# A fused attention and feed-forward block: second layernorm in pairs ahead of q, half of the second v in front of the branch, maxima on two PSUM rings, third layernorm among k

## The chip, the cores and the metric

The kernel runs on one core of a Trainium2 chip. The metric is the device time of one execution in microseconds (us). The core's engines are TensorE (PE; its weight loads are listed as PEld), VectorE (DVE), ScalarE (ACT), GpSimd (POOL) and SyncE (SP, which here issues nearly all DMA). Each runs its own instructions in the order of the program and waits on semaphores for the others.

## The reference

The input x is 16 batches of 512 tokens by 512 channels, in float32. There is one block of a transformer with "sandwich" layernorms:

```python
x = x + layernorm(attention(layernorm(x), Wq, bq, Wk, bk, Wv, bv, Wo, bo))
x = x + layernorm(ffn(layernorm(x), gate_w, up_w, down_w, gate_s, up_s, down_s))
```

Attention has 32 heads of 16 channels, two rotary turns of q and k (they are one fixed rotation per token), a causal mask and a softmax over 512 keys. The feed-forward part computes `silu(g) * u` with `g = (x @ gate_w.T) * gate_s` and `u` likewise, over 1408 hidden channels, then the down product times `down_s`. The weights of the feed-forward part are drawn from -1, 0 and 1.

## The kernel before, in words

**The parts.** `front` (line 765) does the first layernorms and batch 0's q, k and v. Then the program branches (line 845), and `batches` (line 863) does everything else. In the branch that runs here, the feed-forward products take each float32 operand as a sum of two rounded parts (`exact`). The branch is taken on a flag: `check_weights` (line 193) rounds each of the 22 weight pieces on ACT and compares on DVE (11 pieces of 128x1024 for gate and up, 11 of 128x512 for down), then `total` adds up the differences, and each engine reads the flag from memory. The pieces are loaded by `load_checks` (line 170) into places that are free at first, `ht` and `xntfl` among them.

**A q or k block** (`qk_block`, line 326) makes 128 channels for 512 tokens: four products on TensorE, each a pair of records in the trace (`pq`, `pk`). ACT then writes `ys` (the bias added, halves swapped), DVE `ya`, POOL multiplies `ys` by the sine. That is the block's tail; `rest` adds the two on DVE, rounds on ACT to `yh`, and takes the remainder on POOL as `yl`; `store` sends both to DRAM (`qd`, `kd`). `ya` and `ys` have one buffer each, so the next block's tail waits for this one's rest.

**A layernorm of 128 tokens**: `stats` (line 235) has three instructions on DVE and two on POOL (a power, `ln_rstd`, and a shift, `ln_sh`). Then one instruction writes `xn`, on DVE in `front` and on ACT (`scaled`) later. `turn` (line 253) transposes it with four products `px` on TensorE, and ACT copies them out to `xnta` (or `xntf`).

**In the front** the second batch's layernorm is spread over the first batch's four q blocks: each block is followed by a check, a layernorm, and three more checks. The second batch's `xn`, transposed, goes to DRAM (`xn1`) and is read back behind the branch. TensorE's products pass through `ps_d`, three PSUM buffers in turn.

**Steps.** Behind the branch the work is a list of steps, six for each group of four heads, eight groups per batch (`one_step`, line 749). A step issues, for a group, a sixth of the score products: those of `st` (keys by queries, for the exponentials `pt`), and those of `s` of the next group but one or the next (queries by keys, for the row maxima `nm`). `s` and `st` each have one buffer of two PSUM banks (`ps_s`, `ps_t`). DVE masks and reduces each `s` (`maxima`, line 606); once per group the maxima are transposed (`pm`) and sent by SP to where the `st` products of that group read them (`mx`). ACT's exponentials are masked on POOL, then multiplied by v (`av`). The steps of n = -2 and n = -1 are a ramp: they have `s` alone, for the first two groups.

**The lists.** Into each step, after the scores, `run_list` (line 691) puts a share of a list of dense work, by cost: 1 for a product, 0.15 for a transpose. In the list, `merge` places a function after so much cost, and `("need", key)` forces a named one. The first list, `dense(0) + ffn_list(None, 2)`, makes v, q and k of batch 1, a product of the biases (`fold_bias`, `po`), and at its end the third batch's layernorms and transposes one after the other. It is spread over 58 of the 60 steps of the ramp and batch 0. The lists after it, for batches 1 to 15, hold the next batch's v, q and k and the previous batch's output product and feed-forward part.

**Loads.** SP issues all loads and stores in program order, and each waits for its own buffers and data: `load_group` (q, kh, kl of one group) at the first step of two groups earlier, weights `w` (four buffers), the copies `wgs` of the gate and up weights, maxima and stores between them. One that waits holds up all that follow.

Of the kernel before, what the change touches and what calls it, by code (L numbers as in the profile page):

```python
# [18 lines left out]
P = 128  # L19
T = 512  # L20
# [34 lines left out]
class Block:  # L55
# [53 lines left out]
    def constants(self):  # L109
        nc, a, con = self.nc, self.a, self.const  # L110
        for tb in range(NB):
            self.load_x(0, tb, ("x", "xr")[tb // 2], 2)
        ncol = sum(n for _, n in a["cols"][1])
        cols = con.tile([P, ncol], FP, tag="cols", name="cols")
        self.sp.dma_start(out=cols, in_=a["cols"][0])
        self.col, at = {}, 0
        for name, n in a["cols"][1]:
            self.col[name] = cols[:, at : at + n]
            at += n
        turn = con.tile([P, 2, T], FP, tag="turn", name="turn")  # L120
        self.cos, self.sin = turn[:, 0, :], turn[:, 1, :]
        nc.scalar.dma_start(out=turn, in_=a["turn"])
        for name in "qk":
            for half in range(2):
                self.load_w(0, name, half)
        for tb in range(NB):
            self.load_x(1, tb, "x1", 4)
        self.ident = con.tile([P, P], FP, tag="ident", name="ident")
        make_identity(nc, self.ident)
        self.neghalf = con.tile([P, 1], FP, tag="neghalf", name="neghalf")  # L130
        nc.gpsimd.memset(self.neghalf, -0.5)
        self.row = {}
# [14 lines left out]
        self.v17 = []  # L147
        for i in range(2):
            t = con.tile([P, NB, WIDTH], FP, tag=f"v17_{i}", name=f"v17_{i}")
            self.v17.append(t)  # L150
        self.one = con.tile([P, P], FR, tag="one", name="one")
        nc.vector.memset(self.one.bitcast(FP), 1.0)
        self.qd, self.kd, self.od, self.rd = [], [], [], []
        for par in range(2):
            for c in range(NC):
                self.qd.append(self.dram.tile([P, 2, T], FP, tag=f"qd{par}{c}", name="qd"))
                self.kd.append(self.dram.tile([2, P, T], FP, tag=f"kd{par}{c}", name="kd"))
                self.od.append(self.dram.tile([8 * 32, T], FP, tag=f"od{par}{c}", name="od"))
                self.rd.append(self.dram.tile([8, T], FP, tag=f"rd{par}{c}", name="rd"))
        self.wgs = self.dram.tile([self.NF, P, 2, NC, P], FP, tag="wgs", name="wgs")  # L160
        self.wds = self.dram.tile([self.F, C], FP, tag="wds", name="wds")
        self.wd = con.tile([P, self.NF, C], FR, tag="wd", name="wd")
        self.xn1 = self.dram.tile([P, NC, T], FP, tag="xn1", name="xn1")
        self.odd = con.tile([P, 2 * self.NF], FP, tag="odd", name="odd")
        self.flag = con.tile([1, 1], mybir.dt.int32, tag="flag", name="flag")
        self.ones = con.tile([P, 1], FP, tag="ones", name="ones")
        nc.vector.memset(self.ones, 1.0)


    def load_checks(self):  # L170

        a, n = self.a, 2 * NC * P
        ht = self.tile([P, self.NF, T], "ht", bufs=1).rearrange("p f t -> p (f t)")
        xl = self.tile([P, NC, T], "xntfl", bufs=1).rearrange("p c t -> p (c t)")
        places = [ht[:, ts(i, n)] for i in range(self.NF * T // n)] + [xl[:, ts(i, n)] for i in range(NC * T // n)]
        small = [tag for tag, k in (("oc", 4), ("q2", 3), ("kh", 3), ("kl", 3)) for _ in range(k)]
        self.wgu0, self.wd0 = [], []

        def load(f):
            w = places.pop() if 3 <= f < 10 else self.tile([P, n], "wf", bufs=3)  # L180
            self.sp.dma_start(out=w, in_=a["wgu"][f].rearrange("p w c j -> p (w c j)"))
            self.wgu0.append(w)

        for f in range(self.NF):
            if f < 10:
                load(f)
            tag = small.pop()
            w = self.tile([P, C], tag, bufs=4 if tag == "oc" else 3)
            self.sp.dma_start(out=w, in_=a["wd"][ts(f, P), :])
            self.wd0.append(w)  # L190
        self.load_check_10 = load

    def check_weights(self):

# [5 lines left out]

        def gate_up(f):
            if f == 1:
                self.load_check_10(10)
            w = self.wgu0[f]
            check(f, w, self.tile(list(w.shape), "pt", bufs=4, dtype=FR))

# [7 lines left out]
            self.pe.matmul(p[0:1, 0:1], n, self.ones, start=True, stop=True)  # L214
            self.dve.tensor_copy(self.flag, p[0:1, 0:1])

        return [lambda f=f, g=g: g(f) for f in range(self.NF) for g in (gate_up, down)] + [total]

    def load_x(self, b, tb, tag="x", bufs=2):
        t = self.tile([P, C], tag, bufs=bufs)  # L220
# [32 lines left out]
    def turn(self, tiles, key, tb, to, big):  # L253
# [3 lines left out]
        def go(c):  # L257
# [3 lines left out]
            if c == NC - 1:  # L261
# [7 lines left out]
                    self.dve.tensor_tensor(lo, p, hi, ALU.subtract)  # L269
                    return  # L270
                if tb == 0:
                    to[key] = self.tile([P, NC, T], big, bufs=1)
                self.act.copy(to[key][:, :, ts(tb, P)], p)

        return [(TR, lambda c=c: go(c)) for c in range(NC)]
# [217 lines left out]
    def dense(self, b):  # L493
# [10 lines left out]
            self.merge(L, rest, 3)  # L504
            self.merge(L, store, 5.5)

        if b == 0:
            do(self.load_xn1)
            for half in range(2):
                do(self.load_w, 1, "v", half)  # L510
        if nxt:
            for tb in range(NB):
                L += self.v_block(bn, tb)
                if b == 0 and tb < 2:
                    do(self.load_w, 1, "q", tb)
            for c in range(NC):
                if c < 2:
                    do(self.load_w, o, "o", c)
# [20 lines left out]
        for c in range(NC):  # L539
# [6 lines left out]
                    self.merge(L, later[c], 5, ("f", c + 2))  # L546
            if nxt:
                qk("k", c)
        if not old:
            L += self.fold_bias()  # L550
        return L


# [10 lines left out]
            ks.append(t)  # L564
        self.qs[n], self.ks[n] = q, ks

    def scores(self, n, m, third, pair):

        ps = pm = None
        todo = []  # L570
        if 0 <= n < self.B * NG:
# [11 lines left out]
                        (out, self.one[r2, :], mx[r2, T - w : T], False, True),  # L583
                    ]
        if 0 <= m < self.B * NG:
            pm = self.ps_s.tile([P, 2, T], FP, tag="s", name="s")
            q, ks = self.qs[m], self.ks[m]
            for jj in range(2):
                j = 32 * (2 * (1 - pair) + jj)
# [159 lines left out]
    def one_step(self, work, n, i):  # L749
# [2 lines left out]
        third, pair = divmod(i, 2)  # L752
        if i == 0 and n + 2 < self.B * NG:
            self.load_group(n + 2)
        self.scores(n, n + 2 if third >= 1 else n + 1, third, pair)
# [9 lines left out]
    def front(self):  # L765
# [8 lines left out]

        def norm(b, tb):
            xt = self.xts.pop((b, tb))
            r, sh = self.stats(xt)

            def rest():
                xn = self.xns[("a", b), tb] = self.tile([P, C], "xn", bufs=2)  # L780
                self.dve.tensor_scalar(xn, xt, r, sh, ALU.mult, ALU.add)

            return rest

# [10 lines left out]
            rest = now  # L795
        rest()
        turn(0, NB - 1)
        for t in self.v17:
            self.pool.memset(t, 0.0)
            self.pool.memset(t[:, :, DH : H * W : W], 1.0)  # L800
        rests, pending = [], []
        for name in "qk":
            for c in range(NC):
                items, rest, store = self.qk_block(0, name, c)
                for _, f in items[:2]:
                    f()
                for f in pending:
                    f()
                for _, f in items[2:3]:
                    f()  # L810
                for f in rests:
                    f()
                items[3][1]()
                rests, pending = [rest, store], []
                if name == "q":
                    check(1)
                    r = norm(1, c)
                    check(1)
                    r()
                    pending = [lambda c=c: turn(1, c)]  # L820
                    check(2)
                else:
                    check(4)
            if name == "q":
                for half in range(2):
                    self.load_w(0, "v", half)
            else:
                t = self.xnts.pop(("a", 1))
                self.sp.dma_start(out=self.xn1, in_=t)
        for f in rests:  # L830
            f()
        check(len(checks))
# [2 lines left out]
        for tb in range(NB):  # L835
            for _, f in self.v_block(0, tb):
                f()
            if tb == 0:
                checks.pop(0)()

    def run(self):
        self.front()
# [19 lines left out]

    def batches(self):
        B = self.B
        L = self.dense(0) + self.ffn_list(None, 2)
        if self.exact:
            for f in range(self.NF):
                L.insert(8 + 5 * f, (0, lambda f=f: self.sp.dma_start(out=self.wgs[f], in_=self.a["wgu"][f])))
        work = self.run_list(L, 58)
        for n in (-2, -1):  # L870
            for i in range(STEPS):
                self.one_step(work, n, i)
        for b in range(B):
            if b:
# [71 lines left out]
```

## Time and profile before

| | |
|---|---|
| median of 3 runs | 3362.67 us (3357.67 to 3367.87) |
| the profiled execution's own time | 3362.85 us |
| its span, first to last instruction | 3360.9 us |
| PE busy | 3143.6 us (94% of the span) |
| DVE busy | 2057.0 us (61%) |
| ACT busy | 1528.9 us (45%) |
| POOL busy | 1360.9 us (40%) |
| mean granted TensorE clock | 0.969 |

Times in the timeline count from the start of the span. Its lines give start, length, engine, operation, output and inputs, and in square brackets how long the engine was idle before, and what ended that. Lines of waits give who waited for whom: us in total, times, the longest. Lines of stages give a stretch, its length, the busy time of PE, PEld, DVE, ACT and POOL with their instructions, the granted clock of TensorE as a share of full speed, the busy share of the DMA engines and the GB/s moved. In the strip of the page, each digit is a fortieth of the span (84 us): busy tenths, or tenths of the full clock. Almost every instruction is issued through one helper, line 50, so groups are told apart by their tiles.

### The profile page before, as it was taken

The numbers are of one execution on the slowest core, as the hardware profiler recorded it, in microseconds if no ns is written. First come the engines' busy times: TensorE is split into PE (matmuls) and PEld (weight loads), VectorE is DVE, ScalarE is ACT, GpSimd is POOL, SyncE is SP. The second block draws the span as 40 slices with busy tenths as digits, with TensorE's granted clock in tenths as the row PEclk, the third lists the DMA queues.
The fourth block names the chain that finished last, engine by engine and source line by source line (L and its number), as shares of the span: only waits on it lengthen the run. The fifth ranks groups of instructions, "written<-read, shape, count | busy, mean of one in ns | idle before, by whom it ended". The sixth has DMA issues, their size and how long they took to land. (4 is left out here: it accounts for less than half of the span.)

```text
span 3360.9 us, 56842 instructions
## 1 busy us (share of the span) xinstructions
PE 3143.6 (94%) x21258; PEld 1741.6 (52%) x21258; DVE 2057.0 (61%) x3611; ACT 1528.9 (45%) x2239; POOL 1360.9 (40%) x1934
## 2 busy tenths in 40 slices
PE   5787999999999999999999999999999999998867
PEld 2333464645556464554646455564645556464536
DVE  5454766656576665657666665766656576665522
ACT  4243545445454544445454444545444454543322
POOL 3132544343444434344443434444343444433242
PEclk8888999999999999999999999999999999997888
DMA  5444434535244453525445352534535253442321
GB/s 210 155 145 130 159 133 149 171 118 190 93 162 138 144 165 123 190 88 162 140 146 164 121 190 92 166 133 146 168 118 186 94 166 131 141 132 88 118 80 64
DMA packets 227420, 471.24 MB, mean 140 GB/s; under 512 B 40976, under 2 KB 45072, under 8 KB 226704
## 3 DMA queue, kind: packets, MB, share of 16 engines
q1 hardware_dynamic: 226704, 466.47, 41.9%
q8 instruction: 170, 2.79, 0.3%
q14 instruction: 114, 0.93, 0.1%
q10 hardware_dynamic: 432, 1.05, 0.1%
HBM read 345.79 MB, written 125.30 MB: 140 GB/s over the span
## 5 line engine op out<-in xcount | busy, mean ns | idle before, releaser
L50 ACT ACTIVATE pt<-st 128x1024 f32<-128x1024 f32 (+1 forms) x768 | 676.4, 881 | 794.0 <-PE st L50 786.2
L50 DVE TENSOR_REDUCE nm<-s 128x2 f32<-128x256 f32 (+3 forms) x1024 | 821.4, 823 | 26.4
L50 POOL TENSOR_SCALAR_AFFINE_SELECT pt<-pt 128x256 f32<-128x256 f32 (+1 forms) x768 | 371.7, 484 | 1145.0 <-ACT pt L50 1138.6
L50 DVE TENSOR_TENSOR s<-s,mask 128x256 f32<-128x256 f32 (+1 forms) x768 | 396.9, 517 | 568.7 <-PE s L50 513.0
L50 PE MATMUL st<-q,kh 32*128 32x512 f32 (+3 forms) x2048 | 414.4, 401 | 33.9 <-ACT pt L50 32.8
L50 PEld LDWEIGHTS st<-q,kh 32*128 32x128 f32 x2048 | 193.0, 185 | 465.7 <-issue 235.0
L50 PE MATMUL s<-kh,q 32*128 32x128 f32 (+3 forms) x2048 | 403.6, 402 | 32.1 <-DVE nm L50 23.0
L50 PE MATMUL av<-pt,v 128*32 128x512 f32 (+3 forms) x4096 | 365.3, 452 | 0.0
L50 PE MATMUL s<-kl,q 32*128 32x128 f32 (+3 forms) x2048 | 335.6, 323 | 15.0 <-DMA kl<-kd 15.0
L50 PE MATMUL st<-q,kl 32*128 32x512 f32 (+3 forms) x2048 | 339.1, 327 | 0.0
L50 PE MATMUL st<-mx,one 2*128 2x512 f32 (+3 forms) x2048 | 336.0, 323 | 0.0
L50 POOL TENSOR_TENSOR hl<-ht,hh 128x512 fp32r<-128x512 f32 (+1 forms) x192 | 229.2, 1194 | 206.0 <-ACT hh L50 185.2
L50 PE MATMUL pd<-wd,hl 128*128 128x512 f32 x704 | 286.8, 407 | 2.8 <-POOL hl L50 2.8
L50 PE MATMUL pg<-xntf,wf 128*128 128x512 f32 x704 | 287.9, 409 | 1.3 <-ACT xntf L50 1.3
L50 PE MATMUL pd<-wd,hh 128*128 128x512 f32 x704 | 288.1, 409 | 0.0
L50 PE MATMUL pu<-xntfl,wf 128*128 128x512 f32 x704 | 284.5, 404 | 0.0
L50 PE MATMUL pu<-xntf,wf 128*128 128x512 f32 x704 | 284.5, 404 | 0.0
L50 PE MATMUL pg<-xntfl,wf 128*128 128x512 f32 x704 | 282.1, 401 | 0.0
L50 PE MATMUL pv<-w,xnta 128*128 128x512 f32 x512 | 256.5, 633 | 11.7 <-DMA w<-in_wv 10.6
L50 PE MATMUL po<-w,oc 128*128 128x512 f32 x512 | 245.5, 614 | 17.4 <-DMA w<-in_wo 17.4
L50 POOL TENSOR_TENSOR yl<-ya,yh 128x512 fp32r<-128x512 f32 x128 | 163.1, 1274 | 235.4 <-ACT yh L50 235.4
L50 PE MATMUL pk<-xnta,w 128*128 128x512 f32 x512 | 254.8, 616 | 2.2 <-DVE ya L50 2.2
(100 smaller groups left out, 4966.8 us busy)
## 6 DMA issues: line engine op xcount, KB each, us to landing
wf<-wgs SPq DMA_DIRECT2D x176, 512.0 KB
q<-qd SPq DMA_DIRECT2D x128, 256.0 KB
kh<-kd SPq DMA_DIRECT2D x128, 256.0 KB
kl<-kd SPq DMA_DIRECT2D x128, 256.0 KB
od<-ot SPq DMA_DIRECT2D x128, 256.0 KB
w<-in_wo SPq DMA_DIRECT2D x34, 512.0 KB
xr<-in_x SPq DMA_DIRECT2D x66, 256.0 KB
w<-in_wq SPq DMA_DIRECT2D x32, 512.0 KB
```

The costliest lines, as they stand in the source:

```text
L50: return self.tc.keep_in_program_order(f(*args, **kwargs))
```

## The change

- **Front, loads.** The second batch's x is loaded ahead of k's weights; all 11 gate and up pieces are loaded ahead of the 11 down pieces, and are checked first.
- **Front, second layernorm.** Its first two tiles are done as a pair ahead of q's blocks, the other two behind q's first and second block, with `xn` written on ACT. The transposes follow each q block. Fewer checks stand behind each block (three behind the first two, then two), so that three are left after the last k block.
- **Front, v.** The memsets of the v buffers come with the constants. The flag is now computed behind the third of batch 0's v blocks, where it was behind the first. Two of batch 1's four v blocks are done ahead of the branch, from `xntf` and with batch 0's v weights.
- **Ramp.** The first group is loaded at once, and the ramp begins at its third step (ten steps; the two left out had no scores). In the ramp every other `s` uses the buffer of `st`.
- **First list.** A list of its own, `first_list`: batch 1's other two v blocks, q and k, with the third batch's layernorms and transposes one behind each k block, into `ht`. It is spread over 56 steps. The weights of the third batch's v and q are loaded at its end, its first x tiles before q.

```diff
@@ constants
-        for name in "qk":
-            for half in range(2):
-                self.load_w(0, name, half)
+        for half in range(2):
+            self.load_w(0, "q", half)
         for tb in range(NB):
             self.load_x(1, tb, "x1", 4)
+        for half in range(2):
+            self.load_w(0, "k", half)
...
             t = con.tile([P, NB, WIDTH], FP, tag=f"v17_{i}", name=f"v17_{i}")
+            nc.gpsimd.memset(t, 0.0)
+            nc.gpsimd.memset(t[:, :, DH : H * W : W], 1.0)
@@ load_checks
+        for f in range(self.NF - 1):
+            load(f)
         for f in range(self.NF):
-            if f < 10:
-                load(f)
@@ check_weights
-        return [lambda f=f, g=g: g(f) for f in range(self.NF) for g in (gate_up, down)] + [total]
+        return [lambda f=f, g=g: g(f) for g in (gate_up, down) for f in range(self.NF)] + [total]
@@ turn
-                    to[key] = self.tile([P, NC, T], big, bufs=1)
+                    to[key] = self.tile([P, self.NF if big == "ht" else NC, T], big, bufs=1)[:, 0:NC, :]
@@ scores
-            pm = self.ps_s.tile([P, 2, T], FP, tag="s", name="s")
+            if n < 0 and i % 2:
+                pm = self.ps_t.tile([P, 2, T], FP, tag="st", name="st")
+            else:
+                pm = self.ps_s.tile([P, 2, T], FP, tag="s", name="s")
@@ front
+        r = [norm(1, 0), norm(1, 1)]
+        check(1)
+        for f in r:
+            f()
...
                 if name == "q":
-                    check(1)
-                    r = norm(1, c)
-                    check(1)
-                    r()
-                    pending = [lambda c=c: turn(1, c)]
-                    check(2)
-                else:
-                    check(4)
+                    if c < 2:
+                        turn(1, c)
+                        r = norm(1, c + 2)
+                        check(1)
+                        r()
+                    else:
+                        turn(1, c)
+                check(2)
...
-            if tb == 0:
+            if tb == 2:
                 checks.pop(0)()
+        self.wts[1, "v", 0], self.wts[1, "v", 1] = self.wts[0, "v", 0], self.wts[0, "v", 1]
+        for tb in range(2):
+            for _, f in self.v_block(1, tb):
+                f()
@@ new
+    def first_list(self):
...
+        do(self.load_xn1)
+        for half in range(2):
+            do(self.load_w, 1, "v", half)
+        for tb in range(2, NB):
+            L += self.v_block(1, tb)
...
+        for c in range(NC):
+            st = {}
+
+            def first(c=c, st=st):
+                st["rest"] = self.norm_1(2, c)
+
+            do(first)
+            self.merge(L, lambda st=st: st["rest"](), 2, ("a", c))
+            qk("k", c)
+            L.append(("need", ("a", c)))
+            L += self.turn(self.xns, ("a", 2), c, self.xnts, "ht")
+        L += self.fold_bias()
+        for k in range(4):
+            do(self.load_w, 2, "vq"[k // 2], k % 2)
@@ batches
-        L = self.dense(0) + self.ffn_list(None, 2)
...
-        work = self.run_list(L, 58)
-        for n in (-2, -1):
-            for i in range(STEPS):
+        work = self.run_list(self.first_list(), 56)
+        self.load_group(0)
+        for n, i0 in ((-2, 2), (-1, 0)):
+            for i in range(i0, STEPS):
                 self.one_step(work, n, i)
```

More of the change, by code (lines that the diff above doesn't have):

```diff
@@ L179, in load @@
         def load(f):
-            w = places.pop() if 3 <= f < 10 else self.tile([P, n], "wf", bufs=3)
+            w = places.pop() if 3 <= f < self.NF - 1 else self.tile([P, n], "wf", bufs=3)
             self.sp.dma_start(out=w, in_=a["wgu"][f].rearrange("p w c j -> p (w c j)"))
             self.wgu0.append(w)
+        for f in range(self.NF - 1):
+            load(f)
         for f in range(self.NF):
-            if f < 10:
-                load(f)
             tag = small.pop()
@@ L190, in load_checks @@
             self.wd0.append(w)
-        self.load_check_10 = load
+        self.load_last = lambda: load(self.NF - 1)
     def check_weights(self):
@@ L202, in gate_up @@
             if f == 1:
-                self.load_check_10(10)
+                self.load_last()
             w = self.wgu0[f]
@@ L505, in qk @@
             self.merge(L, store, 5.5)
[L507 to L510, printed above, removed]
         if nxt:
@@ L513, in dense @@
                 L += self.v_block(bn, tb)
-                if b == 0 and tb < 2:
-                    do(self.load_w, 1, "q", tb)
             for c in range(NC):
@@ L548, in dense @@
                 qk("k", c)
-        if not old:
-            L += self.fold_bias()
         return L
@@ L565, in load_group, with scores @@
         self.qs[n], self.ks[n] = q, ks
-    def scores(self, n, m, third, pair):
+    def scores(self, n, m, i):
+        third, pair = divmod(i, 2)
         ps = pm = None
@@ L754, in one_step @@
             self.load_group(n + 2)
-        self.scores(n, n + 2 if third >= 1 else n + 1, third, pair)
+        self.scores(n, n + 2 if third >= 1 else n + 1, i)
         if i == 2 and 0 <= n + 1 < self.B * NG:
@@ L776, in norm @@
             xt = self.xts.pop((b, tb))
-            r, sh = self.stats(xt)
+            mr = self.stats(xt)
             def rest():
                 xn = self.xns[("a", b), tb] = self.tile([P, C], "xn", bufs=2)
-                self.dve.tensor_scalar(xn, xt, r, sh, ALU.mult, ALU.add)
+                if b == 0:
+                    self.dve.tensor_scalar(xn, xt, mr[0], mr[1], ALU.mult, ALU.add)
+                else:
+                    self.scaled(xn, xt, mr)
             return rest
@@ L797, in front @@
         turn(0, NB - 1)
[L798 to L801, printed above, removed]
+        r = [norm(1, 0), norm(1, 1)]
+        check(1)
+        for f in r:
+            f()
+        rests = []
         for name in "qk":
@@ L806, in front @@
                     f()
[L807 to L810, printed above, removed]
                 for f in rests:
                     f()
-                items[3][1]()
-                rests, pending = [rest, store], []
+                for _, f in items[2:]:
+                    f()
+                rests = [rest, store]
                 if name == "q":
-                    check(1)
-                    r = norm(1, c)
-                    check(1)
-                    r()
-                    pending = [lambda c=c: turn(1, c)]
-                    check(2)
-                else:
-                    check(4)
+                    if c < 2:
[3 more added lines that the diff above has]
+                        r()
+                    else:
+                        turn(1, c)
+                check(2)
             if name == "q":
@@ L827, in front @@
             else:
-                t = self.xnts.pop(("a", 1))
-                self.sp.dma_start(out=self.xn1, in_=t)
+                self.sp.dma_start(out=self.xn1, in_=self.xnts["a", 1])
         for f in rests:
@@ L837, in front, with qk @@
                 f()
-            if tb == 0:
+            if tb == 2:
                 checks.pop(0)()
+        self.wts[1, "v", 0], self.wts[1, "v", 1] = self.wts[0, "v", 0], self.wts[0, "v", 1]
+        for tb in range(2):
+            for _, f in self.v_block(1, tb):
+                f()
+    def first_list(self):
+        L = []
+        do = lambda f, *args: L.append((0, lambda: f(*args)))
+        do(self.load_xn1)
[3 more added lines that the diff above has]
+            L += self.v_block(1, tb)
+        for half in range(2):
+            do(self.load_w, 1, "q", half)
+        for tb in range(2):
+            do(self.load_x, 2, tb)
+        def qk(name, c):
+            items, rest, store = self.qk_block(1, name, c)
+            L.extend(items)
+            self.merge(L, rest, 3)
+            self.merge(L, store, 5.5)
+        for c in range(NC):
+            if c < 2:
+                do(self.load_w, -1, "o", c)
+            qk("q", c)
+            if c % 2:
+                do(self.load_w, 1, "k", c // 2)
+        for c in range(NC):
+            st = {}
[9 more added lines that the diff above has]
+            do(self.load_w, 2, "vq"[k // 2], k % 2)
+        if self.exact:
+            for f in range(self.NF):
+                L.insert(16 + 6 * f, (0, lambda f=f: self.sp.dma_start(out=self.wgs[f], in_=self.a["wgu"][f])))
+        return L
     def run(self):
@@ L864, in batches @@
         B = self.B
-        L = self.dense(0) + self.ffn_list(None, 2)
-        if self.exact:
-            for f in range(self.NF):
-                L.insert(8 + 5 * f, (0, lambda f=f: self.sp.dma_start(out=self.wgs[f], in_=self.a["wgu"][f])))
-        work = self.run_list(L, 58)
-        for n in (-2, -1):
-            for i in range(STEPS):
+        work = self.run_list(self.first_list(), 56)
+        self.load_group(0)
+        for n, i0 in ((-2, 2), (-1, 0)):
+            for i in range(i0, STEPS):
                 self.one_step(work, n, i)
```

## The prediction

> **What bounds the kernel now.** I read the page's slices of the span first.
>
> ```profile
> PE   5787999999999999999999999999999999998867
> ...
> PEclk8888999999999999999999999999999999997888
> ```
>
> TensorE (PE) is busy at 9 tenths or more from the fifth slice (336 us) to near the end, at a full clock. There only less TensorE work would help, and the change takes none away. The first four slices show 5 to 8 tenths and a clock of 0.8: the time to win lies there. Whatever is won before TensorE becomes the bound moves all later work forward by the same amount. So next I cut the start into stages at its landmarks: the group loads behind the branch (97.7), the first `st` score product of batch 0 (140.4), and the first value product of the third batch (307.8), where the TensorE-bound part begins.
>
> ```profile
> core 0: us, PE busy (x) PEld busy (x) DVE busy (x) ACT busy (x) POOL busy (x), PEclk, DMA share, GB/s
> 0.00:97.70 97.70, 61.56 (x130) 28.00 (x130) 45.52 (x98) 40.19 (x58) 34.93 (x46) 0.88 0.57 206
> 97.70:140.40 42.70, 26.28 (x84) 10.12 (x83) 15.96 (x25) 2.01 (x4) 0.00 (x0) 0.72 0.46 170
> 140.40:307.80 167.40, 132.16 (x1006) 55.31 (x1005) 93.19 (x153) 68.75 (x97) 49.95 (x75) 0.85 0.44 141
> 307.80:500.00 192.20, 190.03 (x1330) 106.37 (x1328) 125.69 (x220) 93.84 (x138) 82.40 (x117) 1.00 0.43 142
> ```
>
> The last row is 99% TensorE; the three above have 88, 72 and 85 hundredths of the clock and idle time. What ends that idle time, by the waits of TensorE in 140.4 to 307.8:
>
> ```profile
> PE px L50 <- ACT xn L50: 13.7, 4, 6.2
> PE s L50 <- DVE nm L50: 9.7, 13, 1.4
> PE st L50 <- ACT pt L50: 7.7, 9, 1.6
> PE s L50 <- DMA kh<-kd: 2.7, 1, 2.7
> ```
>
> The first row is the third batch's layernorm, done with nothing beside it. In 97.7 to 140.4 the same view has these:
>
> ```profile
> PE pv L50 <- DMA w<-in_wv: 10.6, 1, 10.6
> PE s L50 <- DVE nm L50: 5.1, 5, 2.0
> ```
>
> Last, the timeline. The first three lines show why the front is slow (one q block's chain crosses ScalarE (ACT), VectorE (DVE) and GpSimd (POOL)), the last two where the 13.7 us lie.
>
> ```profile
> 60.50 1.27 POOL L50 TENSOR_TENSOR ys<-ys,turn 128x512 f32<-128x512 f32 x1 [1.38 <-ACT ys L50]
> ...
> 63.95 0.95 POOL L50 TENSOR_TENSOR ln_rstd<-ln_ve,neghalf 128x1 f32<-128x1 f32 x1 [2.18 <-DVE ln_ve L50]
> ...
> 66.87 14.74 PE L50 MATMUL pk<-xnta,w 128*128 128x512 f32 x28
> ...
> 283.70 0.90 PE L50 MATMUL px<-ident,xn 128*128 128x128 f32 x3 [6.24 <-ACT xn L50]
> ...
> 291.12 1.11 PE L50 MATMUL px<-ident,xn 128*128 128x128 f32 x4 [4.11 <-ACT xn L50]
> ```
>
> **Front, up to the group loads.** `ys` starts for the eight q and k blocks at 24.9, 36.4, 48.0, 59.1, 70.6, 78.1, 83.8 and 88.0: periods of 11.5 four times, then 7.5, 5.8 and 4.2, in all 63.1. After the change the same dependencies give, with durations from the timeline:
> - Start: the v memsets (4.74 on POOL, at 13.97) go ahead of the first layernorm, into 2.1 to 6.9 where POOL waits for x. The fourth `xn`, 2.14 beside them against 0.54 for the first, shrinks by 1.6, so q starts near 16.7 instead of 18.1. Half rate for some 6 us, as now, makes the first block 6.5: `ys` at 23.2. Without that POOL idle time the memsets would delay the first layernorm by up to 4.7.
> - q blocks 1 and 2 (three 128x1024 checks and a layernorm each): ys 1.38, ya 0.75, statistics 1.05, power and shift 1.25, xn on ACT 0.81, two casts 2.10, last compare 1.41, add 0.69, yh 0.62: 10.1, with hops 10.7.
> - q blocks 3 and 4 (two checks): ys 1.38, xntf 0.58, casts 2.10, compare 1.41, add 0.69, yh 0.62: 6.8, with hops 7.2.
> - k blocks (two 128x512 checks of 0.77): ys 1.38, ya 0.75, 1.54, 0.69, 0.62: 5.0, with hops 5.1.
>
> Last `ys`: 23.2 + 2x10.7 + 2x7.2 + 3x5.1 = 74.3. Then its tail to `yl` (6.3) and the store: 82. The last three checks, their sum and the flag end at about 83. SP took 2.0 from its last store (ends 95.67) to the group load (97.67), so the loads start at 85. The checks move from q to after it and q's layernorms pair up; no work is taken away.
>
> TensorE then still has v block 4 and the two moved v blocks of batch 1: 12 products of 0.86 and 2.8 for a cold start: 96.3, and 2.0 for the branch: first `s` at 98.3, against 112.25 now. The wait of 10.6 for `w` is covered by those 7 us of moved v work, not shortened: the load of xnta, issued at 99.4 and used at 108.6, takes 9.2 with wv behind it, and now it must wait for v block 4 to have read xnta (89.5, behind the flag), so it lands at 98.8. Behind it on SP stand wv, group 1's loads, the maxima and wq; TensorE's first v product comes at 99.2, after one score step. That is 0.4 us of margin; without the cover each us late is a us lost. **Gain 14.**
>
> **Ramp (10 score steps to the first `st`).** Now 28.1 us (112.25 to 140.39): `s` has one buffer, so product, mask and reductions alternate. VectorE needs per step 2.02, 1.16 or 1.70 by the three shapes (0.70 + 1.29, 0.43 + 0.69, 0.43 + 1.23), in all 4x2.02 + 4x1.16 + 2x1.70 = 16.1, and 0.3 for `nml`. TensorE needs 7.8 of `s` products (0.85, 0.65 or 0.9 a step) and 8 v products of 1.06: 16.3. With the second ring they overlap; the best case is 16.4, the worst today's 28.1. I take 20, nearer the busy sums, since both engines are nearly full and TensorE may start cold (+3). The maxima reach `mx` through SP 5 to 6 us after their transpose and have 4 steps of 2.0. **Gain 8**: first `st` at 118.
>
> **Batch 0's 48 steps.** Now 167.4. The undisturbed stretch 146.4 to 260.1 has six groups (from the `pm` marks) in 113.7 us: 3.16 a step, with 0.94 dense products in each; 48 steps like that are 151.6. The new list leaves 36 products there (32 of q and k, 4 of the bias) instead of 45: 9 fewer, worth up to 9x1.06 = 9.5 and nothing where `s` waits for `nm`; I take 6. It adds the 16 transposes (0.6 per four: 2.4) and four layernorms (statistics 1.05 on DVE, power and shift 0.83 on POOL, 0.81 and 0.58 on ACT), hidden by the four k products ahead of their transposes (five steps, some 15 us, for a chain of 3.5); in the in-order queues they hold back exponentials and maxima a little: 1 us each, between 0 and the 3.4 each costs today. 151.6 - 6 + 2.4 + 4 = 152. **Gain 15.** This agrees with the other end: 13.7 of waits vanish, and most of the half rate from 283 to 307. The weights of the third batch are now issued at the last list step, just three steps (8 us) before use, and x far ahead; a 512 KB load is about 1.3 us at the 400 GB/s of the start. Stores of k come six steps before the loads that need them.
>
> A rule against this: the Trainium skill, TensorE: Matmul & The Clock Gate, section Part 1, says that the half-rate state comes after an idle window of about 3.4 us and goes after one as busy, so gaps of 1 to 2 us would not matter. The trace differs: at 211 to 219 half rate follows waits of 1.45 and 0.91, and the first q block ran at half rate for 6 us. By the page, only the waits at 283 and 291 cool the clock, the change removes them, and the 0.91 of the stretch (some 20 us at half rate, up to 10 lost) goes too: 142 instead of 152, and 3315 in all. By the row thinner TensorE work keeps such dips. I keep 152.
>
> **Sum.** 14 + 8 + 15 = 37 us, on a profiled execution of 3362.85 us (span 3360.9), 0.2 from the median 3362.67: about 3325.5, so 3325. Behind 307.8 nothing is bought or lost: the third batch's transposed x lies in `ht`, whose next writer, gate_up of batch 0, comes after its last reader in program order.
>
> **Rivals.**
> - The stalls of batch 0 stay (15 in 100). For: the waits for `nm` and `pt` come from in-order queues, and layernorms among k add to them. If each layernorm costs its 3.4 and the fewer products save nothing: 151.6 + 2.4 + 13.7 = 168, gain 22: 3341. Against: the chain of 3.5 has 15 us to run.
> - The loads behind the branch set the ramp (8 in 100): xnta waits for v block 4, and one late load leaves the v products 6 late and the ramp at 28: gain 37 - 14 = 23: 3340. For: 0.4 us of margin. Against: the group 0 loads are out 13 us before they are used.
> - The clock stays full (10 in 100): 3315 as worked out above, or less.
> - The change doesn't do what it says (3 in 100): the longer queues of checks ahead of q's adds keep the front at 97, the ramp stays DVE-bound at 28 by latency, and only the 13.7 go, half into the layernorms: 3355.
> - Slower (5 in 100): half rate through all of batch 0. Its TensorE work at full rate is 8 groups of 8.9 (15.3 less six products of 1.06), 36 products of 1.06 and the transposes: 112 us. At half rate 224, that is 57 more than now against 22 won: 3398. It decides from a granted clock of 112/189 = 0.59 over the stage. For: 0.68 was seen from 260 to 308, with 0.50 for 20 us. Against: that was with waits of 6 and 4 us; the stretch before it had 0.91.
>
> **Numbers.** The likeliest case (59 in 100) is 3325, its own range 3315 to 3335. Leaving out at most 2 in 10: 3308 (clock full, ramp at 16.4) to 3344 (one of the first two rivals in full). About 0.3% (10 us) is what a measurement can tell from no change: faster 0.92, same 0.03, slower 0.05.
>
> **What would show it.** Group loads near 85, first `s` near 98, first `st` near 118, first value product of the third batch near 270; no wait of `px` for `xn` of over 1 us there; `w<-in_wv` gone from TensorE's waits or under 2 us; the 99% stage unchanged in length. Wrong if `ys` still has periods of 11 in q, if the reductions leave VectorE idle in the ramp, or if the clock of batch 0 falls below 0.8.

## The result and the profile after

The changed kernel takes 3320.35 us (median of 4 runs, 3316.29 to 3325.69); the kernel before took 3362.9 us beside it. The ratio is 0.9875, with a 95% interval of 0.9853 to 0.9896: 42.5 us less, where 37 were forecast (3325 us, range 3308 to 3344). Later runs of the same kernel gave a median of 3319.91 (ratio 0.9870, 0.9852 to 0.9888) and a single 3318.42.

The profiled execution, the slowest of the four, took 3325.69 us, span 3324.0. First its slices, 83 us each:

```profile
PE   6889999999999999999999999999999999997867
...
PEclk9899999999999999999999999999999999997888
```

TensorE is at 9 tenths from the fourth slice instead of the fifth, and the rest of the strip is as it was but for one digit near the end. Then the same stages, cut at the same landmarks: group loads, first `st` product, first value product of the third batch. Columns as before: stretch, length, busy PE, PEld, DVE, ACT and POOL with their instructions, granted clock, DMA share, GB/s.

```profile
core 0: us, PE busy (x) PEld busy (x) DVE busy (x) ACT busy (x) POOL busy (x), PEclk, DMA share, GB/s
0.00:83.50 83.50, 53.91 (x125) 24.54 (x126) 43.88 (x94) 43.44 (x62) 34.96 (x46) 0.93 0.66 242
83.50:111.40 27.90, 25.57 (x99) 10.63 (x97) 15.39 (x25) 3.17 (x6) 0.00 (x0) 0.95 0.45 153
111.40:268.20 156.80, 127.16 (x994) 53.33 (x994) 92.99 (x152) 67.71 (x96) 50.03 (x75) 0.87 0.47 160
268.20:460.40 192.20, 190.02 (x1332) 106.37 (x1328) 125.84 (x220) 93.90 (x138) 82.49 (x117) 1.00 0.45 149
```

The last row begins at 268.2 where it began at 307.8, and holds the same work in the same 192.2 us at the same clock: what was won ahead of it, 39.5 us, is still there at 460. From that landmark to the end the two profiled executions differ by 2.7 us (3053.1 and 3055.8), and in all 14 profiles of this study that remainder lies between 3045 and 3057. So the landmark tells the kernels apart more sharply than the whole time does, and I use it below.

The waits of TensorE in batch 0's stage (who waits for whom: us in total, times, longest):

```profile
PE s L50 <- DVE nm L50: 12.1, 17, 1.8
PE st L50 <- ACT pt L50: 11.7, 13, 2.1
PE s L50 <- DMA kh<-kd: 4.1, 2, 3.2
```

The 13.7 us of `px` for `xn` are gone. The waits for maxima and exponentials have grown from 9.7 and 7.7. From the timeline, ACT's last `ys` of the front, the v products behind the flag, the first group load among them, the first `s`, and the one long wait in batch 0's stage:

```profile
73.17 1.38 ACT L50 ACTIVATE ys<-pk,cols 64x512 f32<-64x512 f32 x2
...
81.98 5.40 PE L50 MATMUL pv<-w,xnta 128*128 128x512 f32 x8
...
83.46 0.33 SPq L50 DMA_DIRECT2D q<-qd  x1
...
87.22 7.03 PE L50 MATMUL pv<-w,xntf 128*128 128x512 f32 x16
94.18 0.33 PE L50 MATMUL s<-kh,q 32*128 32x128 f32 x2
94.34 0.27 PE L50 MATMUL s<-kl,q 32*128 32x128 f32 x2
...
119.37 0.33 PE L50 MATMUL s<-kh,q 32*128 32x128 f32 x2 [3.25 <-DMA kh<-kd]
```

`ys` starts at 22.7, 33.3, 43.9, 50.7, 57.4, 62.7, 67.9 and 73.2. The first `s` stands right behind the v products, and the wait of 10.6 us for `w` is gone: from 83.5 to 111.4 the view of TensorE's waits has this line alone.

```profile
PE st L50 <- DVE nm L50: 2.3, 3, 0.9
```

### The profile page after: what moved, and what is told of

The parts are those of the page before. It is cut to its first block, busy times and chain, and to the rows that moved or that the text cites. A ratio compares the mean times of both kernels' runs of the same rounds, so it can differ in the third digit from the quotient of the medians.

```text
span 3324.0 us, 56844 instructions
## 1 busy us (share of the span) xinstructions
PE 3130.9 (94%) x21258; PEld 1736.3 (52%) x21258; DVE 2054.3 (62%) x3607; ACT 1533.1 (46%) x2243; POOL 1362.6 (41%) x1934
## 5 line engine op out<-in xcount | busy, mean ns | idle before, releaser
L50 DVE TENSOR_REDUCE nm<-s 128x2 f32<-128x1024 f32 (+1 forms) x1017 | 816.1, 824 | 26.3
L50 PE MATMUL s<-kh,q 32*128 32x512 f32 (+1 forms) x2034 | 399.8, 400 | 30.9 <-DVE nm L50 20.1
L50 PE MATMUL s<-kl,q 32*128 32x512 f32 (+1 forms) x2034 | 332.2, 322 | 15.9 <-DMA kl<-kd 15.9
L50 PE MATMUL po<-w,oc 128*128 128x512 f32 x512 | 245.2, 613 | 17.5 <-DMA w<-in_wo 17.5
L50 ACT CAST hh<-ht 128x512 fp32r<-128x512 f32 (+1 forms) x192 | 111.8, 583 | 279.4 <-PE pd L50 211.2
L50 PE MATMUL pk<-xnta,w 128*128 128x512 f32 x480 | 238.8, 616 | 2.0 <-DVE ya L50 2.0
```

Source lines behind the costliest of these rows:

```text
L50: return self.tc.keep_in_program_order(f(*args, **kwargs))
```

## The experiments

Three kernels undo one part of the change, one moves v behind the branch, one makes one part alone, and the others measure a disputed cost. This table has the landmarks of one profiled execution each (us), the granted clock in the ramp, and the measured time. The ramp runs from the first `s` to the first `st`, batch 0's stage from there to the third batch's first v product, which is "the landmark" below. A ring is a PSUM buffer for scores: with one ring the ramp's `s` all go through the buffer of `s`, with two they alternate with that of `st`.

| kernel | first `s` | ramp | clock in ramp | batch 0's stage | third batch's first v product | median us, ratio to before |
|---|---|---|---|---|---|---|
| before | 112.3 | 28.1 | 0.74 | 167.4 | 307.8 | 3362.9 |
| changed | 94.2 | 17.2 | 1.00 | 156.9 | 268.2 | 3320.35, 0.9875 |
| changed, again | 93.4 | 17.7 | 0.93 | 158.8 | 269.9 | 3319.91, 0.9870 |
| changed, third | 93.2 | 17.2 | 1.00 | 159.7 | 270.1 | 3318.42, one run |
| one ring in the ramp | 93.9 | 29.4 | 0.59 | 157.9 | 281.2 | 3329.68, 0.9897 |
| third layernorm at the end | 93.1 | 17.6 | 0.94 | 168.8 | 279.5 | 3336.22, 0.9915 |
| front in the old order | 104.6 | 29.7 | 0.58 | 158.2 | 292.4 | 3336.99, 0.9910 |
| all of v behind the branch | 86.7 | 34.8 | 0.61 | 153.3 | 274.8 | 3326.48, 0.9875 |
| ring alone, on the kernel before | 111.5 | 17.4 | 1.00 | 165.6 | 294.5 | 3352.02, 0.9959 |
| one ring, ramp filled | 94.1 | 25.8 | 1.00 | 155.2 | 275.1 | 3333.96, one run |
| third group loaded early | 92.9 | 17.7 | 0.93 | 156.0 | 266.6 | 3316.96, 0.9873 |
| 16 products more | 93.6 | 23.7 | 0.61 | 156.8 | 274.1 | 3326.07, 0.9896 |
| no mask in batch 0's stage | 93.9 | 23.6 | 0.62 | 141.4 | 258.9 | 3308.17, one run |
| v last | 86.5 | 17.5 | 0.66 | 160.3 | 264.3 | 3318.36, 0.9868 |

**One ring in the ramp.**

```diff
-            if n < 0 and i % 2:
-                pm = self.ps_t.tile([P, 2, T], FP, tag="st", name="st")
-            else:
-                pm = self.ps_s.tile([P, 2, T], FP, tag="s", name="s")
+            pm = self.ps_s.tile([P, 2, T], FP, tag="s", name="s")
```

> The changed kernel, but in the ramp every s product goes through the one ring of s again. Theory (the second ring overlaps products and reductions; that is the ramp's gain of 10.9 us, from 28.1 to 17.2): the ten steps go back to about 28 us, the first st to about 122 us instead of 111.4, the time to about 3331 us. Rival (the ramp was shortened by the loads being there and by a warm clock, not by the ring): the ramp stays under 21 us, first st under 115, time 3320 to 3324.

The theory holds in the length: 29.4 us, first `st` at 123.3, and the landmark 11 to 13 us later. The ratio's interval, 0.9868 to 0.9925, overlaps that of the changed kernel; the landmark is what decides. But the clock in the ramp fell as well, from full to 0.59. The stages from the first `s` on, first this kernel's, then, in its own fence, that of the kernel with a filled ramp (below):

```profile
93.87:123.28 29.41, 24.03 (x74) 9.67 (x74) 15.96 (x25) 1.43 (x3) 0.00 (x0) 0.59 0.30 114
```

```profile
94.14:119.91 25.77, 24.12 (x95) 10.08 (x95) 15.96 (x25) 1.43 (x3) 0.00 (x0) 1.00 0.28 106
```

**One ring, with the ramp filled,** to part waits from half rate.

```diff
...
         self.scores(n, n + 2 if third >= 1 else n + 1, i)
+        if n < 0:
+            p = self.ps_av.tile([P, T], FP, tag="av", name="av")
+            self.pe.matmul(p, self.ident, self.cos, start=True, stop=True)
```

> The changed kernel with one ring in the ramp, and with one product more in each ramp step (128x128 by 128x512, into the PSUM bank of av, read by nobody), to fill TensorE's waits. Theory (the 29.4 us of the ramp with one ring are half waits for the reductions, half the half rate of 0.59 that these waits bring): clock over 0.85 and ramp 22 to 26 us in spite of 10 products more. Rival (the wait for the one buffer is all): ramp 28 us or more.

With ten products more, the ramp is 3.6 us shorter: TensorE's waits for the maxima in it fall from 5.4 to 1.6 us, and its clock is full (second fence). That the waits halved the clock in the run before is not shown by this pair: two executions with two rings and shorter waits had half rate as well (last section), and each of the two kernels has one profile. Compared at a like clock, one ring instead of two costs 5.7 us at half rate (29.4 against 23.7 and 23.6) and up to 8.6 at full rate (25.8, fillers included, against 17.2). So of the 12.2 us between the two profiles about half is the difference in clock.

**The ring alone, on the kernel before.**

```diff
-            pm = self.ps_s.tile([P, 2, T], FP, tag="s", name="s")
+            if n < 0 and pair:
+                pm = self.ps_t.tile([P, 2, T], FP, tag="st", name="st")
+            else:
+                pm = self.ps_s.tile([P, 2, T], FP, tag="s", name="s")
```

> The kernel before with one part of the change alone: in the ramp every other s uses the buffer of st. Theory (the ring is worth its 11 to 12 us by itself): ramp near 17 us instead of 28.1, time about 3351 us. Rival (the ring pays only where TensorE comes into the ramp warm; here it waits 10.6 us for w behind the branch and runs at half rate, as in the run with the old front, where two rings took 29.7 us at a clock of 0.58): ramp 26 us or more, time 3359 or more.

The ramp is 17.4 us and the time 3352.02 (ratio 0.9959, 0.9946 to 0.9971): 13 us less than the kernel before, over twelve executions, with an interval of 10 to 18. The part stands alone; it needs neither the new front nor v blocks ahead of the branch. The rival wasn't put to the test: TensorE waited 9.2 us for `w` behind this branch and its clock was at half from 101.4 to 111.6, but it was full again when the ramp began at 111.5.

**The front in the old order** (loads, checks, memsets and second layernorm as before; two v blocks of batch 1 still in front).

```diff
...
-        r = [norm(1, 0), norm(1, 1)]
-        check(1)
-        for f in r:
-            f()
...
-                    if c < 2:
-                        turn(1, c)
-                        r = norm(1, c + 2)
-                        check(1)
-                        r()
-                    else:
-                        turn(1, c)
-                check(2)
+                    check(1)
+                    r = norm(1, c)
+                    check(1)
+                    r()
+                    pending = [lambda c=c: turn(1, c)]
+                    check(2)
+                else:
+                    check(4)
...
```

> The changed kernel, but the front has the loads, checks, v memsets and second layernorm in the order of the kernel before; half of the second v stays in front of the branch, and the flag stays behind the third v block. Theory (the gain of the front lies in the shorter chain from one block's ys to the next): ys of the eight blocks at 24.9 to 88 again, group loads at about 97.5 instead of 83.5, first s at about 108, time about 3334 us. Rival (the front's end is set by TensorE's v products behind the flag, so that the chain's 14 us are partly hidden): first s no later than 101, time 3327 or less.

The group loads are back at 98.4, the first `s` comes 10.4 us late, and the median of 3336.99 is near the 3334 foretold. The order of the front is worth its 10 us. The profiled execution, the slowest of its runs (3345.51), lost 12.5 more in the ramp: the v products behind the branch waited, and then the whole ramp ran at 0.58.

```profile
PE pv L50 <- DMA w<-in_wv: 4.2, 1, 4.2
```

**All of v behind the branch.**

```diff
-        self.wts[1, "v", 0], self.wts[1, "v", 1] = self.wts[0, "v", 0], self.wts[0, "v", 1]
-        for tb in range(2):
-            for _, f in self.v_block(1, tb):
-                f()
...
-        for tb in range(2, NB):
+        for tb in range(NB):
             L += self.v_block(1, tb)
```

> The changed kernel, but all four v blocks of batch 1 stand behind the branch, in the list of 56 steps; so the first list holds 8 products more. Theory (the two blocks cost nothing in front, where they cover the loads behind the branch, and the products they take out of batch 0's stage are worth about 0.7 us each): the wait for w or xnta behind the branch is back with 5 to 8 us, first st within 2 us of 111.4, the stage of batch 0 about 5 us longer than 156.8, time about 3326 us. Rival (in batch 0's stage TensorE has idle time for 8 products anyway): stage within 2 us of 156.8 and time 3317 to 3322; if also the first s comes 7 us earlier without a wait, the time falls to 3314.

The wait for `w` is back with 5.1 us, as foretold: in front the two blocks do cover it. The rest of the theory missed. The first `st` came at 121.5, not near 111.4, because the wait and ten v products instead of eight fell into a ramp at half rate; and the stage of batch 0 was shorter (153.3), not 5 us longer. In time the kernel can't be told from the changed one (both ratios 0.9875). So the half of v in front is worth at most the 5 to 7 us by which the landmark moved, and no measured time shows it. What fell here was the price I put on a product in batch 0's stage; the next kernel asks for it alone.

**16 products more in batch 0's stage.** The first product of each q and k block of batch 1 is done three times.

```diff
...
+            for _ in range(times - 1 if i == 0 else 0):
+                self.pe.matmul(st["p"], lhs(i), rhs(i), start=True, stop=True)
             self.pe.matmul(st["p"], lhs(i), rhs(i), start=(i == 0), stop=(i == n - 1))
...
```

> The changed kernel, but the first product of each of the eight q and k blocks of batch 1 is done three times (the last one counts), so that batch 0's stage holds 16 products more, at the same places. Theory (in that stage TensorE's work is worth about two thirds of its time, as 6 of 9.5 us were taken in the forecast): stage about 157 + 16 x 0.65 = 167 us. Rival (the chain of product, mask and reduction sets the stage, TensorE has room): stage 155 to 160; with a fuller TensorE the clock may rise over 0.87 and the stage may even shrink.

The rival wins in the stage, which takes 156.8 us, no longer than with 16 fewer (156.9 to 159.7 in three executions). TensorE was busy for 136 us instead of 127 to 132, in time that was idle before; and its clock was 0.91 instead of 0.84 to 0.87, so part of the room came from less half rate. The ramp, whose code is that of the changed kernel, was 23.7 us at a clock of 0.61, which moved the landmark (last section). The median is 6 us above the changed kernel's, though the intervals of the ratios overlap. In the profiled execution the ramp accounts for that; the other three have no profile, and their mean clocks (0.973 to 0.978) are no lower than those of the changed kernel (0.973 to 0.977). So a cost of up to 6 us outside this profile's stage is not excluded, where 10 were expected.

**No mask in batch 0's stage.**

```diff
-        self.dve.tensor_tensor(diag, diag, mask, ALU.add)
+        if not self.bare:
+            self.dve.tensor_tensor(diag, diag, mask, ALU.add)
...
+        self.bare = 0 <= n < NG
```

> The changed kernel without the additions of the mask to s in batch 0's 48 steps (the maxima are then taken over future keys too). Theory (the chain of s product, mask and reduction through one buffer sets the stage): 48 x 0.52 us leave the chain, the stage falls from 156.9 to 132 to 142 us. Rival (the in-order queues of ACT and POOL behind the q and k blocks set it, by the waits for pt): stage 150 or more.

The stage falls by 15 to 18 us, to 141.4, of the 24 us of VectorE work taken out (93.0 to 69.0 us busy). The waits for the maxima fall from 12.1 to 5.0 us, those for the exponentials stay:

```profile
PE st L50 <- ACT pt L50: 11.0, 13, 1.6
PE s L50 <- DVE nm L50: 5.0, 8, 1.5
```

So VectorE's work on the scores, and not TensorE's, sets much of batch 0's stage. The fewer waits for maxima fit a chain of score product, mask and reduction through one buffer; but the run relieves VectorE's whole queue, and none gave `s` a second buffer in this stage, so that it is the buffer is argued, not shown.

**The third layernorm at the end of the list again.**

```diff
         for c in range(NC):
+            qk("k", c)
+        L += self.fold_bias()
+        for k in range(4):
+            do(self.load_w, 2, "vq"[k // 2], k % 2)
+        for c in range(NC):
             st = {}
...
-            self.merge(L, lambda st=st: st["rest"](), 2, ("a", c))
-            qk("k", c)
+            self.merge(L, lambda st=st: st["rest"](), 4, ("a", c))
             L.append(("need", ("a", c)))
             L += self.turn(self.xns, ("a", 2), c, self.xnts, "ht")
-        L += self.fold_bias()
-        for k in range(4):
-            do(self.load_w, 2, "vq"[k // 2], k % 2)
```

> The changed kernel, but the third batch's layernorms and transposes stand at the end of the first list again, one after the other behind the bias product, into the same place ht. Theory (their bare chain, shown as 13.7 us of waits of px for xn and most of the half rate after it, is what the change hides): px waits for xn 10 to 14 us again, first value product of the third batch at about 280 instead of 268.2, time about 3332 us. Rival (among k they hold up exponentials and maxima about as much as they cost bare, or the waits before came only from x being loaded late): first value product within 3 us of 268, time 3317 to 3323.

The theory holds: the wait is back, although x was loaded early here, and the landmark is 9 to 11 us later (median 3336.22).

```profile
PE s L50 <- DVE nm L50: 11.5, 13, 1.7
PE px L50 <- ACT xn L50: 11.1, 4, 4.1
```

**The third group loaded early,** to take away the wait of 3.25 us at 119, and the half rate behind it, which the profile of the changed kernel shows as 0.59 in the 20 us from 121:

```profile
121.00:141.00 20.00, 17.95 (x104) 7.00 (x102) 9.07 (x16) 6.23 (x9) 3.72 (x6) 0.59 0.28 93
```

```diff
-        if i == 0 and n + 2 < self.B * NG:
+        if i == 0 and n and n + 2 < self.B * NG:
             self.load_group(n + 2)
+        if i == 0 and n == -1:
+            self.load_group(2)
```

> The changed kernel, but the loads of the third group (q, kh, kl) are issued a step-group earlier, right behind those of the second, ahead of the maxima, wq, x, wo and the first wgs copy on SP. Theory (the miss of batch 0's stage, 156.9 us against 152 foretold, is the new wait of s for kh of 3.2 us at 119 and the half rate that follows it to 137): no such wait, no granted clock of 0.59 in the 20 us behind it, stage near 150, first value product of the third batch near 261, time about 3313 us. Rival (the waits for nm and pt, 24 us in the stage, set its length and another one takes the room): stage 155 or more, time 3318 to 3323.

The rival wins: the wait is gone, but the stage takes 156.0 us. Waits for exponentials and maxima take its place, and half rate is no rarer (0.86):

```profile
PE st L50 <- ACT pt L50: 12.2, 14, 2.1
PE s L50 <- DVE nm L50: 11.7, 16, 1.8
PE s L50 <- DMA kh<-kd: 1.8, 1, 1.8
```

**v last.** If TensorE has room in batch 0's stage, the second v need stand neither in front nor in the ramp.

```diff
...
-        self.wts[1, "v", 0], self.wts[1, "v", 1] = self.wts[0, "v", 0], self.wts[0, "v", 1]
-        for tb in range(2):
-            for _, f in self.v_block(1, tb):
-                f()
...
             L += self.turn(self.xns, ("a", 2), c, self.xnts, "ht")
-        L += self.fold_bias()
+        for tb in range(NB):
+            L += self.v_block(1, tb)
...
-        work = self.run_list(self.first_list(), 56)
+        work = self.run_list(self.first_list(), 46)
...
-                self.one_step(work, n, i)
+                self.one_step(iter(()), n, i)
+                if (n, i) == (-1, 0):
+                    self.load_xn1()
+                    for half in range(2):
+                        self.load_w(1, "q", half)
```

> Built on the changed kernel: no product of batch 1's v in front or in the ramp; all four v blocks stand at the end of the first list, which is spread over batch 0's 46 steps alone (1.18 products a step); the bias product stands behind q; the first three groups, xnta and wq are loaded at once. Theory (TensorE has free room in batch 0's stage, 16 products more cost nothing there, so the 7 us of v in front can move into it): first s at 86 to 87 without a wait, ramp 17 to 21, stage 155 to 160, first value product of the third batch at 258 to 266 instead of 266.6 to 268.2, time 3310 to 3318. Rival (16 more on top of the denser list make TensorE the bound of the stage, or the ramp without products runs at half rate): first value product at 268 or later, time 3320 or more.

The first `s` comes at 86.5, the ramp takes 17.5 us (even at a clock of 0.66, as it has little TensorE work left), and the stage 160.3 with 52 products instead of 36. The landmark is at 264.3, 4 to 6 us ahead of the changed kernel's. The time, 3318.36 against 3319.91 on the same chip (ratios 0.9868 and 0.9870 with intervals of 0.002 to each side), is not told apart from it. It beats the kernel before clearly, and the changed one only by the landmark.

**The changed kernel, twice more.**

> The changed kernel once more, unaltered, on one chip with the next runs. Theory (the half rate in a ramp comes and goes with the clock's own windows: the run with 16 products more had a ramp of 23.7 us at a clock of 0.61 with the same code up to there): the landmarks as before up to the first s (94), the ramp 17 to 24 us, the stage of batch 0 155 to 158. Rival (the clock follows from the code alone): ramp 17.2 again within 0.5.

> The changed kernel a third time, one look, for the spread of the ramp and of batch 0's stage: ramp 17 to 24 us if the half rate there is a matter of chance, 17.2 if it follows from the code; stage 155 to 158.

Both had a fast ramp (17.7 and 17.2), and stages of 158.8 and 159.7: the first profile's 156.9 lay at the low end. By these two alone the half rate would seem to follow from the code; two other kernels with the same code up to the end of the ramp speak against it (last section).

## Why the prediction was right

The forecast had the time and the places of the gains, but not their order: it put batch 0's stage first, and the front won most. Of its three terms two were too small (by 4.1 and 2.9 us) and one too large (by 4.5). That the sum came within 5 us owes something to their cancelling.

- **Front (14 foretold, 18.1 measured).** The chain from block to block was right nearly to the us: `ys` at 22.7 to 73.2 for 23.2 to 74.3, group loads at 83.5 for 85. That its order alone is worth 10 us is shown by the front in the old order. Too dear were two steps of TensorE behind the flag, which itself came 1 us early: the 12 products took 12.2 us (5.4 and 7.0, with no gap) instead of 13.1, and "2.0 for the branch" was SP's price, put on TensorE; its own first `s` followed at once. The 0.4 us of margin for the loads held: no wait for `w`.
- **Ramp (8 foretold, 10.9 measured).** 17.2 us for 20: nearly the VectorE sum of 16.1. I had added for a cold start that didn't come in this execution. Two executions in which the half rate did come had 23.6 and 23.7, so the range of 16.4 to 28.1 was a fair one, and 20 lay between the two real cases.
- **Batch 0's stage (15 foretold, 10.5 measured).** The step that failed is "9 fewer, worth up to 9x1.06 = 9.5 and nothing where s waits for nm; I take 6". The count was off: the stage of the kernel before has 83 records of such products (11 of `pv`, 32 of `pq`, 32 of `pk`, 8 of `po`), two to a product, so about 41 and not 45; the 45 counts transposes and two steps that have no list work. And fewer products won nothing: with the layernorms at the end, 36 of them took 168.8 us, where 41 took 167.4 (the kernel before) and 165.6 (the ring alone). Nor did 16 more make the stage longer. Without that term the sum reads 151.6 + 2.4 + 4 = 158.0, and the three profiles of the changed kernel have 156.9, 158.8 and 159.7. What the stage won comes from the layernorms: placed at the end again, the stage takes 168.8.
- **The rule on the clock.** The row was the better guide. From the page's idle window of about 3.4 us the prediction took that only such gaps bring half rate, and that the stage would be 142 us at a full clock. That reading is narrower than the section, which also tells of a kernel whose frequent short waits made the clock swing. The changed kernel has one wait of about that length (3.25 us); with it taken away, no wait over 2.1 us was left and the clock was still 0.86.
- **Rivals.** "The stalls of batch 0 stay" came half true: fewer products saved nothing, as it said, but the layernorms hid well. Half rate through all of the stage did not come (0.84 to 0.87). The loads behind the branch did not set the ramp, but do when the two v blocks are taken from in front of them (5.1 us) and when the front is late (4.2).

## What to carry to other kernels

Before pricing a product that a list spreads over steps, ask which engine's chain sets those steps: where TensorE waited in them, as in batch 0's stage, 16 products more left the length as it was, and five fewer won nothing. Where product, mask and reduction alternate through a single buffer, look for a second one that lies idle in that phase: here one condition in the code was worth 13 us. Short waits can come with half rate and so cost more than their length; but how much, one profile doesn't tell. And to tell a change of tens of us in a start-up from noise, compare landmarks in the profiles and keep the long, equal remainder out of the comparison, with more than one execution, because half rate alone moved a ramp by 6 us.

## What the runs showed of the hardware

**Half rate that isn't set by the code alone.** Six executions have the same instructions on every engine through nearly all of the ramp: three of the changed kernel, and those with the third layernorm at the end, with 16 products more and without the mask. The ramp took 17.2, 17.7, 17.2 and 17.6 us in the first four, and 23.7 and 23.6 in the other two. The same wait of 0.8 us stands in each of the two shown here, first with 16 products more, then, in its own fence, in the changed kernel:

```profile
98.58 0.39 PE L50 MATMUL st<-kh,q 32*128 32x256 f32 x2 [0.83 <-DVE nm L50]
```

```profile
99.16 0.39 PE L50 MATMUL st<-kh,q 32*128 32x256 f32 x2 [0.82 <-DVE nm L50]
```

Three stretches of the execution with 16 products more show what followed:

```profile
93.00:100.00 7.00, 6.17 (x31) 2.75 (x30) 5.39 (x10) 0.59 (x1) 0.00 (x0) 0.92 0.37 143
100.00:107.00 7.00, 7.00 (x14) 2.00 (x12) 3.70 (x5) 0.59 (x1) 0.00 (x0) 0.50 0.00 0
107.00:118.00 11.00, 10.87 (x40) 4.79 (x41) 6.50 (x12) 0.84 (x2) 0.00 (x0) 0.50 0.47 167
```

and the same stretches of the changed kernel:

```profile
93.00:100.00 7.00, 6.18 (x32) 2.74 (x31) 4.84 (x9) 0.59 (x1) 0.00 (x0) 1.00 0.45 175
100.00:107.00 7.00, 6.94 (x34) 2.76 (x33) 6.43 (x11) 0.84 (x2) 0.00 (x0) 1.00 0.00 1
107.00:118.00 11.00, 7.35 (x38) 2.83 (x37) 7.44 (x12) 2.63 (x3) 0.82 (x2) 1.00 0.76 280
```

Once the clock had halved, near 99, it stayed so until 122.8, although TensorE's records fill 17.87 of the 18 us shown in the last two stretches. The section of the Trainium skill that the prediction drew on has half rate end after some 3.4 us of work; here it didn't. In this phase about half of the work (7.8 of 16.3 us by the forecast's sum) is score products on 32 rows of the array, and whether that has a part in it was not tried.

What makes one execution halve its clock and another not stays open, but the traces narrow it down. In all 14 of them the records of the granted clock are only ever full or half, and it changes only at points of a grid of 3.41 us, which lies differently against the program in each execution. The first `s` comes 1.2, 1.8 and 2.0 us behind such a point in the three of the changed kernel and 1.8 with the third layernorm at the end; it comes 1.5 and 1.3 behind in the two that halved. How busy TensorE was between two points doesn't decide it: 2.58 of the 3.41 us ahead of the halving with 16 products more, and 2.59 in the stretch with the same wait in the changed kernel, whose clock stayed full. A start at a different place in the grid would fit, but two cases of six don't show it.
